# Feed-forward stage of a Mamba block: a written table of slots in place of the scheduler from the third group on, and an earlier place for W_down

## The chip, the core and the metric

The kernel runs on one core of one Trainium2 chip. The metric is the device time of one execution in microseconds (us), where lower is better; the time before is the median of three runs.

## The reference

The block takes 8192 rows of 512 values. The first part is a Mamba layer (a scan over a state of 16 per channel); the change does not touch it. The second part is a feed-forward network whose inputs and weights are rounded to a 4-bit grid (FP4) in blocks of 16, each block with its own scale:

```python
def fp4_quant_dequant(x):            # BLOCK = 16, along the last axis
    scale = jnp.maximum(jnp.max(jnp.abs(xb), axis=-1, keepdims=True) / 6.0, 1e-12)
    xn = xb / scale
    idx = jnp.searchsorted(_MID, jnp.abs(xn))
    return (_GRID[idx] * jnp.sign(xn) * scale).reshape(shape)
...
h = _layernorm(x, axis=-1) * (1 + cb) + sb      # x: 8192 x 512
gate = fp4_linear(h, w_gate)                    # 512 -> 1408
y    = fp4_linear(h, w_up)
x = x + gb * fp4_linear(silu(gate) * y, w_down) # 1408 -> 512
```

## The kernel before

The Mamba layer takes the first two thirds of the time. Its last rows are written to a DRAM buffer `mo`, one of 16 pieces of 512 rows, and the feed-forward stage reads them from there.

The feed-forward stage works in 16 **groups** of 512 rows (`n` from 0 to 15). The 1408 hidden channels are 11 blocks of 128 (`NF` = 11), and these are taken in four **parts** of 3, 3, 3 and 2 blocks (`PARTS`, `FPB` = 3). The tiles hold fp32. For each group:

- `load` and `head` (lines 910 to 927), four times, one for each 128 rows: two loads on the queue of SyncE (SP), the residual sum on GpSimd (POOL), the sums of a layer norm on VectorE (DVE), a power on POOL, the scaling on DVE, two multiply-adds with the modulation on POOL, and then the four steps of the rounding helper `_fp4_steps`: `scales` (DVE: maximum of a block, scale, reciprocal, multiply), `leads` (ScalarE, ACT: two passes), `rounds` (DVE: four passes) and `values` (POOL: multiply by the scale).
- `turn` (line 938), four times: four 128x128 transposes on TensorE (PE), and a copy by ACT into `xqT`, the group's input with channels on the partitions.
- `up` (line 966), eleven times: four matmuls for the gate and four for the other half, into the PSUM tiles `pg` and `pu` (two buffers each); ACT's Silu of `pg`, DVE's product with `pu`, and DVE's transpose within 32x32 blocks into `ht`.
- `quantize` (line 981), four times, one for each part: the same rounding steps on up to 1536 columns, and at the end, in `back`, DVE's transpose into `hT` (line 989). The last part has 1024 columns.
- `down` (line 993), four times: eleven matmuls of `hT` with `wd` into `po`, DVE's sum with the residual (line 1004) and the store.

`quantize_down` rounds a row block of W_down (128 x 1408; four of them, with a row scale `gc` that carries the output gate) and `turn_down` transposes it into `wd`, once, during groups 0 and 1.

One program text issues all this, and for this stage the order on each engine is chosen by the framework's scheduler, by its own estimates and the order of the text as priority. What the text says is that the steps of part `c` are spread over the `up` calls of part `c`+1, that the heads of group `n`+1 are issued with parts 0 and 1 of group `n`, and that the four `down` calls of group `n`-1 come after the **first part** (three `up` calls) of group `n`:

```python
if n > 0 and c == (1 if n == 1 else 0):
    for j in range(NJ):
        down(n - 1, j)
```

The Mamba layer, in contrast, has a written order (`tc.manual_schedule()`), in which each engine executes its instructions as the text issues them.

Of the kernel before, what the change touches and what calls it, by code (L numbers as in the profile page):

```python
# [8 lines left out]
F32 = mybir.dt.float32  # L9
# [12 lines left out]
def _layernorm(nc, small, src, dst, mhalf):  # L22

    st = small.tile([P, 6], F32, tag="st", name="st")
    nc.vector.bn_stats(st, src)
    mv = small.tile([P, 2], F32, tag="mv", name="mv")
    nc.vector.bn_aggr(mv, st)
    ve = small.tile([P, 1], F32, tag="ve", name="ve")
    nc.vector.tensor_scalar(ve, mv[:, 1:2], EPS, None, ALU.add)
    rstd = small.tile([P, 1], F32, tag="rstd", name="rstd")  # L30
    nc.gpsimd.tensor_tensor(rstd, ve, mhalf, ALU.pow)
    nc.vector.tensor_scalar(dst, src, mv[:, 0:1], rstd, ALU.subtract, ALU.mult)
# [69 lines left out]
def mamba_then_fp4_ffn(  # L102
# [768 lines left out]
    with ExitStack() as fa:  # L871
# [3 lines left out]
        FPB = 3  # L875
        PARTS = [(f, min(FPB, NF - f)) for f in range(0, NF, FPB)]
        wq2 = pool("wq2", 1)
        wd = wq2.tile([P, NF, DM], F32, tag="wd", name="wd")
        gc = wq2.tile([P, NK], F32, tag="gc", name="gc")
        hTp = pool("hTp", len(PARTS) + 1)  # L880
        wide = pool("wide", 1)
        work = pool("fwork", 1)
        io = pool("fio", 2 * NJ + 2)
        xqp = pool("xqp", 2)
        fsm = pool("fsm", 2)
        wq = pool("wq", 1, side="right")
# [4 lines left out]
        wu = wq.tile([P, NK, FF], F32, tag="wu", name="wu")  # L891
        sb = wq.tile([P, DM], F32, tag="sb", name="sb")
# [14 lines left out]
        head_work = Wide(work, DM, ("xn", "e"))  # L907
        xts2, xqT, hTs, todo, turned = {}, {}, {}, [], []

        def load(t):  # L910
            xt = io.tile([P, DM], F32, tag="x1", name=f"x1_{t}")
            nc.sync.dma_start(xt, mo[t // NJ][t % NJ * P : (t % NJ + 1) * P, :])
            h2 = work.tile([P, DM], F32, tag="h2", name=f"h2_{t}", bufs=2)
            nc.sync.dma_start(h2, x[t * P : (t + 1) * P, :])
            xts2[t] = xt, h2

        def head(t):

            xt, h2 = xts2[t]
            nc.gpsimd.tensor_tensor(xt, xt, h2, ALU.add)  # L920
            _layernorm(nc, small, xt, h2, mhalf)
            nc.gpsimd.tensor_tensor(h2, h2, cb1, ALU.mult)
            nc.gpsimd.tensor_tensor(h2, h2, sb, ALU.add)
            *steps, values = _fp4_steps(nc, head_work, fsm, h2, None, DM, slope0, nc.vector)
            for step in steps:
                step()
            xts2[t] = xt, values()
# [18 lines left out]

        def quantize_down(r):
            raw = wide.tile([P, FF], F32, tag="wraw", name=f"wraw_{r}")
            nc.sync.dma_start(raw, w_down[r * P : (r + 1) * P, :])

            *steps, values = _fp4_steps(
                nc, rows_work, fsm, raw, None, FF, slope0, nc.gpsimd, gc[:, r : r + 1]
            )

            def keep():
                turned.append((r, values()))

            return [*steps, keep]

        def turn_down():  # L960
            for r, q in turned:
                transposed(q, NF, lambda b0, nb, pt: nc.scalar.activation(
                    wd[:, b0 : b0 + nb, r * P : (r + 1) * P], pt[:, :nb, :], AF.Copy))
            turned.clear()

        def up(n, f, ht, i):
# [9 lines left out]
            g = wide.tile([P, T], F32, tag="g", name=f"g_{n}_{f}", bufs=3)  # L976
# [4 lines left out]
        def quantize(n, c, ht):  # L981
# [3 lines left out]

            def back():
                xn = values()
                hT = hTs[n, c] = hTp.tile([P, FPB * T], F32, tag="hT", name=f"hT_{n}_{c}")
                nc.vector.transpose(hT[:, :w], xn)  # L989

            return [*steps, back]

        def down(n, j):
            t = n * NJ + j
            po = pdn.tile([P, DM], F32, tag="po", name=f"po2_{t}")
            for c, (f0, nb) in enumerate(PARTS):
                for i in range(nb):
                    o = i * T + j * P
                    nc.tensor.matmul(  # L999
                        po, lhsT=hTs[n, c][:, o : o + P], rhs=wd[:, f0 + i, :],  # L1000
                        start=(f0 + i == 0), stop=(f0 + i == NF - 1),
                    )
            xt = xts2.pop(t)
            nc.vector.tensor_tensor(xt, xt, po, ALU.add)
            nc.sync.dma_start(out[t * P : (t + 1) * P, :], xt)

        nc.sync.dma_start(sb, rows[0:1, :].partition_broadcast(P))
        nc.sync.dma_start(cb1, rows[1:2, :].partition_broadcast(P))
        for t in range(NJ):
            load(t)  # L1010
            head(t)
            turn(t)
        for f0, nb in PARTS:
# [3 lines left out]
        nc.sync.dma_start(gc, rows[2:3, :].rearrange("o (r p) -> p (o r)", p=P))  # L1017
        NQ = L // T
        for n in range(NQ):
            for c, (f0, nb) in enumerate(PARTS):  # L1020
                ht = wide.tile([P, FPB * T], F32, tag="ht", name=f"ht_{n}_{c}", bufs=2)
# [5 lines left out]
                turn_down()  # L1027
                todo += quantize(n, c, ht)
                r = n * len(PARTS) + c - 1
                if 0 <= r < NK:  # L1030
                    todo += quantize_down(r)
                if n + 1 < NQ and 0 < c < 3:
                    for j in (2 * c - 2, 2 * c - 1):
                        turn((n + 1) * NJ + j)

                if n > 0 and c == (1 if n == 1 else 0):
                    for j in range(NJ):
                        down(n - 1, j)
                if n + 1 < NQ and c < 2:
                    for j in (2 * c, 2 * c + 1):  # L1040
                        load((n + 1) * NJ + j)
                        head((n + 1) * NJ + j)
        for step in todo:
            step()
        for j in range(NJ):
            down(NQ - 1, j)
# [40 lines left out]
```

## Time and profile before

| | us |
|---|---|
| median of 3 runs (lowest, highest) | 5899.88 (5898.19, 5905.25) |
| the profiled execution, its own time | 5902.15 |
| its span, first to last instruction | 5900.3 |
| first matmul of the feed-forward stage's group 0 | at 3920.88 |
| end of the `down` calls of group 1 | at 4230.12 |
| end of the `down` calls of group 13 | at 5685.27 |
| end of the `down` calls of group 14 | at 5800.32 |

Mean granted TensorE clock of the execution: 0.951. In the profile a matmul in fp32 shows as two instructions, each of a pitch of 0.429 us for a 128x512 tile, so that one `up` is 16 instructions and one `down` is 22. A line of the timeline gives the start, the duration, engine, source line, operation, output and inputs, the count, and in brackets the idle time before it with what ended it. The timeline merges neighbours, and the duration of a merged piece runs to the end of its last instruction, 0.17 us after the next one starts. Line numbers are those of the kernel before.

### The profile page before, as it was taken

Reading aid. Unit: us, or ns where it says so; the run is one execution under the profiler, and the core shown is the slowest. Engines: PE = TensorE matmul, PEld = TensorE weight load, DVE = VectorE, ACT = ScalarE, POOL = GpSimd, SP = SyncE. Lnnn points to the kernel's source line nnn. Section 1 sums busy time; section 2 is a strip of 40 time slices with the busy share of each in tenths; the row PEclk is TensorE's granted clock in tenths of the full one; section 3 lists DMA queues with packets and bytes.
Section 4 is the critical chain, followed back from the end, with each engine's and each line's share of the span. In section 5 each row is a group of like instructions: output and inputs, shape, how many; then the busy total and the mean of one; then the engine's idle time right before and its main releaser. Section 6 shows DMA issues by size and latency. Waiting matters only on the chain.

```text
span 5900.3 us, 58295 instructions
## 1 busy us (share of the span) xinstructions
PE 5272.3 (89%) x19812; PEld 3083.6 (52%) x19812; DVE 5079.0 (86%) x5219; ACT 2985.6 (51%) x5512; POOL 4205.3 (71%) x2419
## 2 busy tenths in 40 slices
PE   7788889889889888898898888788999999999999
PEld 4555556555555655565556555543444444444444
DVE  7999999999999999999999999977777667776674
ACT  6676666776676667667766665522212122211221
POOL 4999999999999999999999999953322323232320
PEclk9999999999999899999999999889999999999999
DMA  5444444444444444444444444430100000000000
GB/s 182 154 155 151 157 152 159 153 154 152 155 158 151 150 157 155 152 154 157 159 153 152 156 150 153 150 113 24 34 22 27 31 28 22 23 27 32 25 15 14
DMA packets 221985, 659.40 MB, mean 112 GB/s; under 512 B 24915, under 2 KB 40403, under 8 KB 221686
## 3 DMA queue, kind: packets, MB, share of 16 engines
q1 hardware_dynamic: 221110, 654.63, 34.1%
q8 instruction: 155, 2.54, 0.2%
q14 instruction: 144, 1.18, 0.1%
q10 hardware_dynamic: 576, 1.05, 0.0%
HBM read 615.22 MB, written 40.38 MB: 111 GB/s over the span
## 4 chain that ended last, share of the span: by engine, by line
DVE 35%; PE 26%; POOL 19%; ACT 10%; issue 9%; DMA 1%; DVEq 0%; POOLq 0%; SPq 0%; ACTq 0%
DVE da L502 13%; POOL db L466 9%; PE po L999 6%; ACT da L476 5%; POOL hp L518 4%; PE pg L972 4%; PE pu L972 4%; DVE hc L526 3%; DVE hp L502 3%; PE po L426 3%; PE y L395 2%; PE cv L271 2%; DVE e L82 2%; PE pz L369 2%; DVE xn L84 2%
## 5 line engine op out<-in xcount | busy, mean ns | idle before, releaser
L466 POOL TENSOR_TENSOR db<-bc,du 128x1024 f32<-128x1024 f32 x1024 | 2395.8, 2362 | 38.0 <-DVE da L502 31.7
L502 DVE TENSOR_TENSOR_SCAN da<-da,state,db 128x512 f32<-128x512 f32 x1280 | 1644.7, 1285 | 91.2 <-ACT da L476 38.1
L476 ACT ACTIVATE da<-delta,na 128x512 f32<-128x512 f32 x2048 | 1407.6, 689 | 427.1 <-DVE hc L526 294.2
L502 DVE TENSOR_TENSOR_SCAN hp<-da,state,db 128x512 f32<-128x512 f32 x768 | 940.8, 1266 | 47.1 <-ACT state L499 27.6
L395 PE MATMUL y<-ident,hc 128*128 128x128 f32 x5120 | 740.0, 294 | 225.9 <-DVE hc L526 184.2
L518 POOL TENSOR_TENSOR hp<-hp,bc 128x1024 f32<-128x1024 f32 x384 | 905.5, 2358 | 30.7
L90 POOL TENSOR_TENSOR xn<-xn,sc 128x512 f32<-128x512 f32 (+3 forms) x144 | 274.8, 1908 | 905.8 <-DVE xn L85 874.2
L395 PEld LDWEIGHTS y<-ident,hc 128*128 128x128 f32 x5120 | 635.1, 151 | 398.4 <-DVE hc L526 245.2
L526 DVE TENSOR_TENSOR hc<-da,bc 128x1024 f32<-128x1024 f32 x640 | 781.3, 1221 | 25.3 <-issue 0.5
L999 PE MATMUL po<-wd,hT 128*128 128x512 f32 x1408 | 636.2, 612 | 57.0 <-DVE hT L989 56.5
L972 PE MATMUL pg<-xqT,wg 128*128 128x512 f32 x1408 | 637.7, 595 | 1.7 <-ACT xqT L943 1.7
L972 PE MATMUL pu<-xqT,wu 128*128 128x512 f32 x1408 | 634.2, 593 | 0.0
L977 ACT ACTIVATE g<-pg 128x512 f32<-128x512 f32 x176 | 102.8, 592 | 833.6 <-PE pg L972 827.3
L369 PE MATMUL pz<-w_in,hT 128*128 128x256 f32 x2048 | 484.4, 391 | 32.7 <-DVE z L384 27.7
L271 PE MATMUL cv<-hT,w_in 128*128 128x512 f32 x1024 | 479.2, 612 | 31.2 <-ACT delta L350 15.8
L999 PEld LDWEIGHTS po<-wd,hT 128*128 128x128 f32 x1408 | 273.8, 196 | 415.5 <-issue 337.0
L426 PE MATMUL po<-w_o,xc 128*128 128x512 f32 x1024 | 463.0, 601 | 18.9 <-DVE z L384 12.2
L299 PE MATMUL cv<-raw,taps 128*128 128x512 f32 x1024 | 467.8, 599 | 12.8 <-ACT taps L285 12.8
L395 PE MATMUL y<-ident,hp 128*128 128x128 f32 x3072 | 447.6, 294 | 27.5 <-POOL hp L518 27.5
L76 ACT ACTIVATE a<-xn 128x512 f32<-128x512 f32 (+3 forms) x144 | 144.5, 1011 | 633.3 <-DVE xn L72 590.1
L395 PEld LDWEIGHTS y<-ident,hp 128*128 128x128 f32 x3072 | 391.9, 153 | 114.7 <-issue 47.7
L972 PEld LDWEIGHTS pu<-xqT,wu 128*128 128x128 f32 x1408 | 267.5, 190 | 335.4 <-issue 327.4
(112 smaller groups left out, 6195.9 us busy)
## 6 DMA issues: line engine op xcount, KB each, us to landing
bc<-bc SPq DMA_DIRECT2D x1024, 512.0 KB, 4.5
x<-in_x_dram SPq DMA_DIRECT2D x64, 256.0 KB, 4.8
h<-in_x_dram SPq DMA_DIRECT2D x64, 256.0 KB, 2.7
x<-mo SPq DMA_DIRECT2D x64, 256.0 KB, 2.7
out_dram<-x SPq DMA_DIRECT2D x64, 256.0 KB, 2.0
mo<-po SPq DMA_DIRECT2D x60, 256.0 KB, 2.2
w_in<-in_w_inT_dram SPq DMA_DIRECT2D x2, 2048.0 KB, 9.2
wm<-in_wmod_dram SPq DMA_DIRECT2D x8, 512.0 KB, 4.4
```

The source lines that it names most:

```text
L271: nc.tensor.matmul(ps, lhsT=w_in[:, f, o : o + P], rhs=hT[k][:, f, :], start=(f == 0), stop=(f == NK - 1),)
L299: nc.tensor.matmul(v, lhsT=taps[:, i, :], rhs=raw[:, i : i + T], start=(i == 0), stop=(i == 3))
L369: nc.tensor.matmul(pz[:, b, :], lhsT=hT[k][:, f, t0 : t0 + P], rhs=w_in[:, f, o : o + DH * P], start=(b == 0 and f == 0), stop=(f == NK - ...
L395: nc.tensor.matmul(y[:, j, i * P : (i + 1) * P], lhsT=src[:, j * P : (j + 1) * P], rhs=ident, start=start and j % 2 == 0, stop=stop, is_tr ...
L426: nc.tensor.matmul(pend["po", k, j], lhsT=xcs[k, d][:, j * P : (j + 1) * P], rhs=w_o[:, d, :], start=(d == 0), stop=(d == ND - 1),)
L466: nc.gpsimd.tensor_tensor(db, bct[slot // DH, 0], dus[k, h, i].unsqueeze(1).to_broadcast([P, GN, T]), ALU.mult)
L476: nc.scalar.activation(pend["da", slot][:, q, :], deltas[k, h][:, i, :], AF.Exp, scale=na[:, d, n : n + 1])
L502: nc.vector.tensor_tensor_scan(to[:, q, :], da[:, q, :], db[:, q, :], state[:, d, n : n + 1], ALU.mult, ALU.add,)
L518: nc.gpsimd.tensor_tensor(to, to, c_rows, ALU.mult)
L526: nc.vector.tensor_tensor(hc, hs, c_rows, ALU.mult)
L972: nc.tensor.matmul(ps, lhsT=wt[:, k, f * P : (f + 1) * P], rhs=xqT[n][:, k, :], start=(k == 0), stop=(k == NK - 1),)
L999: nc.tensor.matmul(po, lhsT=hTs[n, c][:, o : o + P], rhs=wd[:, f0 + i, :], start=(f0 + i == 0), stop=(f0 + i == NF - 1),)
```

## The change

From the third group on (`n` >= 2) the stage has a written order. A group has 15 **slots**: eleven `up` calls, and the four `down` calls of the group before in slots 5 to 8 (`SPLIT` = 5; in the last group they come last). A table says in which slot each other step is issued, after the slot's `up` or `down`; a step's slot may lie in the next group's first five slots. `S`, `L`, `R` and `B` are the steps of a part (scales, leads, rounds with values, and the transpose into `hT`), `n`, `m`, `s`, `l`, `r`, `t` those of a head (residual and norm sums, scaling and modulation, scales, leads, rounds with values, `turn`).

Further: a head's steps for two row blocks alternate (`beside`); its rounded values are written over `h2`, which has four buffers; layer norm is cut in two steps; the residual tile has 11 buffers where it had 10, the Silu's output `g` two where it had three; `hT` has four buffers for the first three parts and one for the last. W_down's row blocks 0 and 1 are loaded behind the first weights and rounded beside group 0's first part (it was blocks 0 to 2 beside parts 1 to 3 of group 0, and block 3 beside part 0 of group 1), and `turn_down` follows a part later. At the end the last group's `down` calls for row blocks 0 and 1 take the parts in turn.

```diff
+        SPLIT, LOADS = 5, (1, 1, 1, 6)
+        PART_STEPS = {"S": (0,), "L": (1,), "R": (2, 3), "B": (4,)}
+        HEAD_STEPS = {"n": (0,), "m": (1,), "s": (2,), "l": (3,), "r": (4, 5)}
+        BESIDE = (4, 5, 6, 7), (10, 11, 12, 14), (13, 14, 15, 17), (16, 17, 18, 19)
+        ENDING = (4, 5, 6, 7), (7, 8, 9, 15), (10, 11, 12, 15), (15, 16, 17, 18)
+        HEADS = 2 * ((5, 6, 7, 7, 8, 11),) + 2 * ((7, 8, 9, 10, 11, 14),)
...
-        hTp = pool("hTp", len(PARTS) + 1)
+        gp = pool("gp", 2)
+        rowsp = pool("rowsp", 3)
+        hTp = pool("hTp", 1)
-        io = pool("fio", 2 * NJ + 2)
+        io = pool("fio", 3 * NJ - 1)
+        hsm = pool("hsm", NJ)
...
         for t in range(NJ):
             load(t)
-            head(t)
-            turn(t)
+        load_down(0)
+        load_weights(0)
+        load_down(1)
+        for c in every[1:]:
+            load_weights(c)
+        beside(head(0), head(1))
+        turn(0)
+        turn(1)
+        beside(head(2), head(3))
+        turn(2)
+        turn(3)
+        todo += quantize_down(0)
+        todo += quantize_down(1)
...
-                turn_down()
-                todo += quantize(n, c, ht)
-                r = n * len(PARTS) + c - 1
-                if 0 <= r < NK:
-                    todo += quantize_down(r)
+                turn_down(ahead)
+                ahead = len(turned)
+                if (n, c) != (1, LAST):
+                    todo += quantize(n, c, ht)
+                if n == 0 and c < 2:
+                    load_down(c + 2)
+                    todo += quantize_down(c + 2)
...
-        for step in todo:
-            step()
-        for j in range(NJ):
-            down(NQ - 1, j)
+        fa.enter_context(tc.manual_schedule())
+        NS = NF + NJ
...
+        for n in range(2, NQ):
+            split = SPLIT if n + 1 < NQ else NF
+            hts = {}
+            for q in range(NS):
+                steps = steps_at.pop(n * NS + q, ())
+                for step in steps:
+                    if step[0] == "t":
+                        do(*step)
+                if split <= q < split + NJ:
+                    down(n - 1, q - split, every)
+                else:
+                    f = q if q < split else q - NJ
+                    c, i = divmod(f, FPB)
...
+                    up(n, f, hts[c], i)
...
+                for step in steps:
+                    if step[0] != "t":
+                        do(*step)
...
+        for some in (every[:1], every[1:2], every[2:3], every[3:]):
+            for j in range(2):
+                down(n, j, some)
+        for j in range(2, NJ):
+            down(n, j, every)
```

## The prediction

> **What bounds the kernel now.** I read the slices of the page first, then the groups, then the timeline of PE between two groups, and last the busy times by stage.
>
> ```profile
> PE   7788889889889888898898888788999999999999
> PEclk9999999999999899999999999889999999999999
> ...
> L999 PE MATMUL po<-wd,hT 128*128 128x512 f32 x1408 | 636.2, 612 | 57.0 <-DVE hT L989 56.5
> ```
>
> The feed-forward stage fills the last 14 slices. In 12 of them PE is over 90% busy, and the only matmuls of the stage with much idle time before them are those of `down`: 57.0 us, waiting for L989, the transpose into `hT`. PE is the bound; what can be won is its pauses. The timeline of PE at one boundary, and then the line of DVE that ends the pause:
>
> ```profile
> 4425.02 3.60 PE L972 MATMUL pu<-xqT,wu 128*128 128x512 f32 x8
> 4428.45 7.89 PE L999 MATMUL po<-wd,hT 128*128 128x512 f32 x18
> 4440.32 33.18 PE L999 MATMUL po<-wd,hT 128*128 128x512 f32 x70 [3.98 <-DVE hT L989]
> 4473.34 3.60 PE L972 MATMUL pg<-xqT,wg 128*128 128x512 f32 x8
> ```
> ```profile
> 4439.04 1.23 DVE L989 STREAM_TRANSPOSE hT<-xn 128x1024 f32<-128x1024 f32 x1
> ```
>
> PE does 18 instructions of `down` (nine matmuls: parts 0 to 2), then stands 3.98 us until the last part's `hT` is there at 4440.27. Afterwards 70 instructions take 33.0 us instead of 70 x 0.429 = 30.0: the granted clock is lower behind the pause. Stage by stage (columns: length, busy PE, PEld, DVE, ACT, POOL, granted clock):
>
> ```profile
> 3920.88:4230.12 309.24, 268.54 (x652) 122.98 (x653) 240.07 (x286) 75.14 (x90) 115.97 (x67) 0.93 0.09 27
> 4230.12:5685.27 1455.15, 1407.11 (x3362) 627.84 (x3361) 1046.18 (x1318) 295.09 (x372) 439.01 (x288) 0.98 0.08 26
> 5685.27:5800.32 115.05, 115.05 (x281) 51.81 (x281) 70.26 (x77) 22.42 (x27) 15.56 (x9) 1.00 0.03 12
> 5800.32:5900.30 99.98, 93.23 (x216) 40.52 (x215) 48.09 (x48) 13.11 (x14) 7.55 (x3) 1.00 0.03 13
> ```
>
> The second row is 12 groups of 121.26 us each. The third is one group in which PE never waited: 115.05, at clock 1.00. It checks by count: 11 `up` x 6.87 + 4 `down` x 9.44 + 4 `turn` x 0.435 = 115.1.
>
> **Part 1: the steady groups.** `down` moves from behind three `up` calls to behind five. The last part's rounding then has two more `up` slots, 13.7 us, against a pause of 4. By the table, counted from the group's start: `R` of the last part is issued in slot 3; DVE reaches it after that slot's product and transpose (0.68 + 0.70), at 27.5 + 0.2 + 1.4 = 29.1, needs 1.23 + 0.65 + 1.22 + 1.22 = 4.3 and ends at 33.4; POOL's multiply (2.25) ends at 35.7; `B` (1.23) comes behind slot 4's `up` and ends at 37.2. The first `down` starts at 34.3 and needs it after nine matmuls, 7.7 us later: 42.0. Margin 4.8 us. So the excess of 121.26 over 115.05, 6.21 us (4 of pause, 2 of clock), goes in all 12 groups: **74.6 us**.
>
> What may be late next is DVE, now in a fixed order. Its work by slot, from the rows of one group: an `up` 1.38, a `down` 0.66, `S` 4.42, `R` 7.15, `B` 1.78 (3.13, 4.32, 1.23 for the last part), a head's `n` 1.0, `m` 0.54, `s` 1.86, `r` 3.04. Slots 0 and 12 come to 8.5 us against a slot of 6.87, slot 11 to 7.5, slot 4 to 7.0; their neighbours have 3 to 6, so DVE falls at most 2.3 us behind (after slot 12) and has caught up by slot 14. PE feels a lag only when an `up`'s product is not done before the matmuls of the second `up` after it fill the same `pu` buffer, 6.87 + 3.43 = 10.3 us later. The `turn` of rows 2 and 3, slot 14 (at 107.3): `r` is DVE work of slot 11, done at 93.6 + 0.2 + 7.5 = 101.3, POOL 1.07, so 102.4; margin 5. The fourth head's load stands on SP behind the store of the second `down` (53.9), lands 2.7 later, and `n` runs after slot 7's `down` (62.7): margin 6. Queued behind that store on SP are only this head's two loads and the next two stores, which nobody waits for before the next group. The extra `hT` and residual buffers cost nothing; two `g` buffers in place of three neither, since a Silu comes 10.3 us after the `up` whose buffer it takes.
>
> DVE and POOL slow each other, though. POOL's multiply L922 has a least time of 1.26 us, a median of 1.27 and a longest of 2.73, which fell beside DVE passes of 1536 columns. One group's 87.2 us of DVE and 37.3 of POOL have the present share of that in them. Taken from both sides: none of POOL's time is added to DVE (87.2 of 115.05), or all of it is (124.5, more than the period). I take the first, as the same work in 121.2 us leaves DVE 28% idle; the second is the rival below.
>
> The Trainium skill (SBUF — State Buffer, "Who interferes with whom") says that DVE instructions with two SBUF inputs and GpSimd instructions that read SBUF exclude one another for a whole instruction. It speaks against a table that puts heads beside parts; by it the period would lie nearer to the second value than I take it.
>
> **Part 2: groups 0 and 1.** The first window holds, for PE, 25 `up` (171.7), 8 `down` (75.5), 8 `turn` (3.5) and W_down's 44 transposes (4.8): 255.5. It took 309.2, so 53.7 are lost: 40.7 of pauses in the timeline (12.5 and 8.3 the longest, mostly for POOL's L90, W_down's and the heads' values) and 13 of clock. After the change the order of each queue can be listed. Three of W_down's four rows are now turned within group 0 and the fourth in the second `up` of group 1 (before: from the end of group 0 to the tenth `up` of group 1). Up to the last pass of the fourth row DVE has, from the first `up` on: 4 rows x 8.4 = 33.5, two parts 26.7, a third part's scales 4.4, three and a half heads 22.5, ten products with transposes 13.8: 101 us. DVE was busy 91% of the time in 3950 to 4100, so 111, and POOL's multiply 2.9: 114. PE has 12.6 `up`, 33 transposes and four `turn` there: 92. So 22 idle. From there to heads 8 and 9: DVE 36 / 0.91 + 1.1 = 40.7 against PE's 31.5: 9 more. Then DVE has slack. With 3 for ACT's copies of W_down through two `pt` buffers it is 34 of pauses, and clock in the old proportion (13 / 40.7), 10: 44. Gain **10 us**; bounds 53.7 (no pause) and -10 (one more wait such as the 12.5).
>
> **Part 3: the two ends.** Before group 0 the loads of `x` for rows 2 and 3 no longer wait for a buffer (they were issued at 3880.86), so the pauses of 5.87 and 3.59 before the third and fourth `turn` shrink; but the four residual sums now stand on POOL ahead of the first head's modulation (two more, 1.27 each). Between -3 and +9.5; I take **2**, near the lower end, since the same PE matmuls of the Mamba layer still follow the first `turn`. At the end, after group 14's last `down`, DVE has the sum 0.66, `B` of parts 1 and 2 3.6, `S` 3.1, `R` 4.3, `B` 1.2, ACT 2.2 and POOL 1.9: 17.1, some 17.7 with hand-overs; PE has 18 matmuls of parts 0 to 2 in that time, 15.4. A pause of 2.3, for 0.79 + 2.40 before: gain **1**.
>
> **Sum.** 74.6 + 10 + 2 + 1 = 87.6. The profiled execution took 5902.15 by its own time (span 5900.3 and 1.85 around it), 2.3 over the median of the runs. 5902.15 - 87.6 = 5814.6, forecast **5815**.
>
> **The rivals.**
> *A wait in the place of the old one.* The heads' values come late and the `turn` of slot 14 (or 11) waits in every group, by DVE's and POOL's fixed order. With the smallest pause of the end stage, 2.4, and 2 of clock, 13 groups give 57: 5872. For it: POOL's two modulations of each head sit between DVE steps. Against: margin 5. Chance 0.12.
> *Slower.* DVE becomes the bound because POOL's instructions hold it up for their full length: 124.5 a group, 13 x (124.5 - 115.05) = 123, so 5938. It is slower than before from the point where more than 121.26 - 87.2 = 34 of POOL's 37.3 us are added. Against: L922's median is its undisturbed time. Chance 0.06.
> *The clock falls when PE no longer pauses.* At 0.98 over 1600 us that is 32: 5847. Against: the third window, 115 us without a pause at 1.00. Chance 0.05.
> *The early stage loses its pauses altogether*: 41 more, 5774. Against: DVE's sum. Chance 0.04.
>
> **How the numbers follow.** 0.73 is left for the forecast, whose own range is 5800 to 5835 (start -3 to +9.5, groups 0 and 1 some 12 either way). To leave out no more than 2 in 10 the range goes up to the first rival: 5795 to 5876. A measurement of this kernel can tell about 0.2%, 12 us. Slower by more 0.06, within 0.01 (a case between the first two rivals), faster 0.93.
>
> **What would show it.** In the changed kernel's profile: periods of 115.1 between the `down` calls of neighbouring groups, no idle time before L1043 (the matmuls of `down`) for `hT`, granted clock 1.00 from group 2 on; 40 to 50 lost before group 2; a pause of 2 to 3 before the last part's matmuls at the end. Wrong would be: pauses before L968 (`turn`) in every group, DVE over 95% busy there, or a period above 117.

## The result, and the profile after

The changed kernel takes 5800.18 us (median of four runs, 5799.56 to 5805.17) against 5899.03 beside it on the same chip: ratio 0.9834, 95% interval 0.9817 to 0.9851. The forecast was 5815 within 5795 to 5876. The profiled execution took 5800.66, span 5798.8, mean granted clock 0.955 (before 0.951).

The page of the changed kernel: the slices of PE and of its clock, and the group of `down`'s matmuls (L999 is now L1043; `turn`'s L935 is L968, `up`'s L972 is L1009).

```profile
PE   7789889888898898888988988768999999999999
PEclk9989999999999999999998999889999999999999
...
L1043 PE MATMUL po<-wd,hT 128*128 128x512 f32 x1408 | 608.5, 593 | 2.0 <-DVE hT L1029 2.0
```

The 57.0 us of idle time before `down` are 2.0, and one of its instructions takes 593 ns in the mean in place of 612: both the pause and the slower clock behind it are gone. The timeline of PE at one boundary shows how:

```profile
4407.08 3.60 PE L1009 MATMUL pu<-xqT,wu 128*128 128x512 f32 x8
4410.51 37.93 PE L1043 MATMUL po<-wd,hT 128*128 128x512 f32 x88
```

All 88 instructions of the four `down` calls come in one piece, where before there were 18, a pause of 3.98 and 70 slower ones. The busy times by stage (columns: length, busy PE, PEld, DVE, ACT, POOL, granted clock, DMA share, GB/s): from the first `up` to the end of group 1's `down`, then twelve groups and a piece, then the end, and last one period by itself:

```profile
3912.18:4218.18 306.00, 281.07 (x685) 127.79 (x686) 243.56 (x273) 75.13 (x91) 106.65 (x59) 0.96 0.07 24
4218.18:5600.46 1382.28, 1382.28 (x3365) 622.52 (x3364) 1111.04 (x1323) 301.89 (x374) 404.43 (x290) 1.00 0.08 28
5600.46:5798.80 198.34, 192.78 (x461) 85.74 (x459) 125.69 (x135) 34.16 (x39) 29.52 (x17) 1.00 0.03 12
4295.46:4410.51 115.05, 115.05 (x281) 51.81 (x280) 92.57 (x110) 25.08 (x31) 33.62 (x25) 1.00 0.08 28
```

In the second row PE is busy for the whole length, at clock 1.00; the period is 115.05. VectorE, which the prediction feared next, is at 92.6 of 115. The end (the 52 instructions from the last part's on) waits 2.04 us:

```profile
5772.70 22.58 PE L1043 MATMUL po<-wd,hT 128*128 128x512 f32 x52 [2.04 <-DVE hT L1029]
```

Where the 101.5 us between the two spans (5900.3 and 5798.8) came from:

| | before | after | gain | predicted |
|---|---|---|---|---|
| last matmul of the Mamba scan (`y`, L395, now L402) | 3869.56 | 3866.71 | 2.9 | not named |
| from there to the first `up` | 51.3 | 45.5 | 5.8 | 2 |
| first `up` to the end of group 1's `down`: lost beyond PE's need (309.24 - 255.5; 306.0 - 269.2, as there are 27 `up` in it, not 25) | 53.7 | 36.8 | 16.9 | 10 |
| from there to PE's last matmul: lost beyond its need | 78.4 | 2.4 | 76.0 | 74.6 + 1 |

The remaining -0.1 is the store at the end. Against the forecast of 5814.6 the profiled execution is 13.9 shorter, which is 2.9 of the first row, 3.8 of the second, 6.9 of the third and 0.3 of the last two. The 2.9 can't be put down to the change: in the 14 executions profiled here that matmul begins anywhere between 3861.4 and 3872.2, with the same text ahead of it, and at 3866.71 and 3864.93 in two executions of the changed kernel. So two kernels are compared below by their ratio and, where less than 0.3% matters, by the time from that matmul to the end of the span: 2030.7 before, 1932.1 and 1932.4 after.

### The profile page after: what moved, and what is told of

It is laid out like the page before. It is cut to its first block, busy times and chain, and to the rows that moved or that the text cites. A ratio compares the mean times of both kernels' runs of the same rounds, so it can differ in the third digit from the quotient of the medians.

```text
span 5798.8 us, 58407 instructions
## 1 busy us (share of the span) xinstructions
PE 5244.5 (90%) x19812; PEld 3077.0 (53%) x19812; DVE 5153.1 (89%) x5219; ACT 2991.1 (52%) x5512; POOL 4168.0 (72%) x2419
## 4 chain that ended last, share of the span: by engine, by line
PE 42%; DVE 24%; POOL 18%; ACT 9%; issue 8%; DMA 0%; DVEq 0%; POOLq 0%; SPq 0%; ACTq 0%
DVE da L509 12%; PE po L1043 10%; POOL db L473 10%; PE pu L1009 9%; PE pg L1009 9%; POOL hp L525 5%; ACT da L483 4%; DVE hc L533 3%; DVE hp L509 3%; PE po L433 3%; PE y L402 2%; PE cv L278 2%; PE pz L376 2%; PE cv L306 1%; POOL du L365 1%
## 5 line engine op out<-in xcount | busy, mean ns | idle before, releaser
L402 PE MATMUL y<-ident,hc 128*128 128x128 f32 x5120 | 737.7, 293 | 223.8 <-DVE hc L533 183.1
L402 PEld LDWEIGHTS y<-ident,hc 128*128 128x128 f32 x5120 | 633.1, 151 | 396.7 <-DVE hc L533 245.2
L97 POOL TENSOR_TENSOR xn<-xn,sc 128x1536 f32<-128x1536 f32 (+2 forms) x80 | 200.6, 2507 | 852.1 <-DVE xn L92 844.7
L1009 PE MATMUL pu<-xqT,wu 128*128 128x512 f32 x1408 | 637.0, 595 | 5.9 <-DVE g L1015 5.9
L1009 PE MATMUL pg<-xqT,wg 128*128 128x512 f32 x1408 | 634.9, 593 | 1.5 <-ACT g L1014 0.8
L1043 PE MATMUL po<-wd,hT 128*128 128x512 f32 x1408 | 608.5, 593 | 2.0 <-DVE hT L1029 2.0
L83 ACT ACTIVATE a<-xn 128x512 f32<-128x512 f32 (+2 forms) x144 | 145.7, 1012 | 869.5 <-DVE xn L79 834.8
L402 PE MATMUL y<-ident,hp 128*128 128x128 f32 x3072 | 449.2, 295 | 27.6 <-POOL hp L525 27.6
L402 PEld LDWEIGHTS y<-ident,hp 128*128 128x128 f32 x3072 | 393.5, 154 | 114.1 <-issue 50.0
L1009 PEld LDWEIGHTS pu<-xqT,wu 128*128 128x128 f32 x1408 | 267.8, 191 | 343.7 <-issue 323.5
L1043 PEld LDWEIGHTS po<-wd,hT 128*128 128x128 f32 x1408 | 268.0, 190 | 339.6 <-issue 330.4
L376 PEld LDWEIGHTS pz<-w_in,hT 128*128 128x128 f32 x2048 | 393.2, 197 | 93.1 <-DVE z L391 32.2
```

What stands on the lines that cost most here:

```text
L376: nc.tensor.matmul(pz[:, b, :], lhsT=hT[k][:, f, t0 : t0 + P], rhs=w_in[:, f, o : o + DH * P], start=(b == 0 and f == 0), stop=(f == NK - ...
L402: nc.tensor.matmul(y[:, j, i * P : (i + 1) * P], lhsT=src[:, j * P : (j + 1) * P], rhs=ident, start=start and j % 2 == 0, stop=stop, is_tr ...
L1009: nc.tensor.matmul(ps, lhsT=wt[:, k, f * P : (f + 1) * P], rhs=xqT[n][:, k, :], start=(k == 0), stop=(k == NK - 1),)
L1043: nc.tensor.matmul(pos[j], lhsT=hTs[n, c][:, o : o + P], rhs=wd[:, f0 + i, :], start=(f0 + i == 0), stop=(f0 + i == NF - 1),)
```

## The experiments

The theory: the pause of PE at every group's `down` goes since `down` is issued two `up` calls later **and** the table keeps VectorE's and POOL's other work from making something else late; VectorE has room; the early stage gains since W_down is ready earlier. The rivals: the place of `down` alone, the order alone, or a VectorE or POOL that is close to being the bound.

| kernel | median, us | ratio to before (95%) | from the last `y` to the end |
|---|---|---|---|
| `down` one part later, nothing else | 5881.89 | 0.9965 (0.9952 to 0.9978) | 2013.7 |
| table, `down` at its old place | 5926.56 | 1.0043 (1.0028 to 1.0058) | 2057.5 |
| after, products turned twice | 5804.44 | 0.9836 (0.9822 to 0.9851) | 1934.4 |
| after, products turned four times | 5946.66 | 1.0077 (1.0060 to 1.0094) | 2081.3 |
| after, heads' values six times | 6134.30 | 1.0393 (1.0375 to 1.0410) | 2259.1 |
| after, 75 short POOL instructions a period | 5803.09 | 0.9830 (0.9813 to 0.9846) | 1938.9 |
| after, W_down at its old places | 5803.72 | 0.9836 (0.9822 to 0.9849) | 1939.2 |
| after, first four heads one by one | 5796.78 | 0.9825 (0.9812 to 0.9839) | 1932.3 |
| after, heads of groups 1 and 2 one by one | 5804.86 | 0.9830 (0.9816 to 0.9845) | 1935.2 |
| after, W_down's rows 2 and 3 a part later | 5799.29 | 0.9829 (0.9816 to 0.9842) | 1928.5 |
| after, once more | 5799.44 | 0.9829 (0.9816 to 0.9843) | 1932.4 |
| after, table from group 1 on | 5792.65 | 0.9813 (0.9798 to 0.9827) | 1924.0 |

### The place of `down` alone

```diff
-                if n > 0 and c == (1 if n == 1 else 0):
+                if n > 0 and c == 1:
```

> The kernel before with one edit: in every group down comes one part later (after the second part, as group 1 has it already); the scheduler still orders all engines and W_down, heads and buffers are as they were. Theory 1 (the record's): a steady period lost 4 us to the wait for hT and 2 us of clock behind it; with down later that wait goes, but the scheduler's order of VectorE's queue lets another wait come up, for the product of the gate that frees pu, so that the period is 116 to 119 us and the whole 5826 to 5874 (middle 118: 5899 - 12 x 3.2 = 5861). Rival: the place of down is everything in the steady groups and the table adds nothing; period 115.0 to 115.6, whole 5826 to 5832. Second rival: the scheduler had down early for a reason, and the wait only changes its name (turn behind POOL's values); period 120 to 122, whole 5885 to 5905.

Measured: 5881.89, a gain of 18 us of the 99. The period is 119.7 (two `down` calls in a row at 4449.74 and 4569.45). The page and the timeline of PE:

```profile
L972 PE MATMUL pu<-xqT,wu 128*128 128x512 f32 x1408 | 656.6, 610 | 35.1 <-DVE g L978 35.0
...
L999 PE MATMUL po<-wd,hT 128*128 128x512 f32 x1408 | 609.3, 594 | 3.2 <-DVE hT L989 3.2
```
```profile
4387.82 5.40 PE L972 MATMUL pu<-xqT,wu 128*128 128x512 f32 x8 [2.68 <-DVE g L978]
```

The wait for `hT` is gone as completely as in the changed kernel (3.2 us in the whole run), and another one stands in its place: PE waits 2.7 us a period for the gate's product, which must read `pu` before it is written again, and then runs eight instructions in 5.40 us that take 3.60 at full clock. VectorE's timeline shows what the product stands behind:

```profile
4378.25 2.45 DVE L82 SCALAR_TENSOR_TENSOR e<-a,e 128x1536 f32<-128x1536 f32 x1
...
4384.47 2.70 DVE L85 SCALAR_TENSOR_TENSOR xn<-e,xn 128x1536 f32<-128x1536 f32 x1
4387.10 0.67 DVE L978 TENSOR_TENSOR g<-g,pu 128x512 f32<-128x512 f32 x1
```

The scheduler put a whole part's rounding, 8.8 us, ahead of it. So the first theory had the right wait, but its size was too small: 2.7 of pause and 1.8 of clock, 4.6 over 115.05, for a range that ended at 4 (and at 5874 for the whole). The rival that the place is everything falls; the second rival's ranges begin at 120 and 5885, just above.

### The table with `down` at its old place

```diff
-        SPLIT, LOADS = 5, (1, 1, 1, 6)
...
-        BESIDE = (4, 5, 6, 7), (10, 11, 12, 14), (13, 14, 15, 17), (16, 17, 18, 19)
+        SPLIT, LOADS = 3, (1, 1, 1, 6)
...
+        BESIDE = (4, 5, 6, 7), (10, 11, 12, 14), (13, 14, 15, 17), (15, 16, 16, 17)
```

> The changed kernel with the table kept but down at its old place, after the first part (slots 3 to 6 of each group; the last part's four steps one slot earlier so that hT can be there at all). Theory: the wait for hT comes back at 4 us or more a period, with up to 2 us of clock behind it, and with the turns of the next group one or two waits besides; period 120 to 125, whole 5860 to 5920. Rival: the order of the queues is what gained, and the table hides the wait even with down early: period 115 to 117, whole 5800 to 5824.

Measured: 5926.56, slower than the kernel before, and 7 above the theory's range; the period is 125.1 (mean of eleven), just above its upper end of 125. One period of PE, its pauses only:

```profile
4363.34 0.66 PE L968 MATMUL pt<-ident,h 128*128 128x128 f32 x4 [0.22 <-POOL h L97]
4366.45 0.75 PE L968 MATMUL pt<-ident,h 128*128 128x128 f32 x4 [2.45 <-POOL h L97]
4426.48 32.88 PE L1043 MATMUL po<-wd,hT 128*128 128x512 f32 x76 [3.58 <-DVE hT L1029]
```

The wait for `hT` is back at 3.57 to 3.95, and two turns wait for POOL besides. It is not quite the old wait: PE does 12 instructions of `down` ahead of it, not 18, so it's the third part's `hT` that is late. VectorE makes it at 4424.69, behind the last part's rounding, which the edit moved two slots earlier while the third part's `B` kept its slot. The turns' wait I put down to the heads' steps of slots 7 and 8, which now stand behind an `up` with its product on VectorE, where they stood beside a `down`; no run takes it apart. A fixed order is only as good as its slots; this one is worse than the scheduler's, and what a table laid out for the old place would give, no run shows. So neither half, as tried here, gains much alone: 18 us and -26 us against 99 together.

### Room on VectorE

```diff
-            nc.vector.transpose(ht[:, i * T : (i + 1) * T], g)
+            for _ in range(2 if n > 1 else 1):       # and 4 in the second kernel
+                nc.vector.transpose(ht[:, i * T : (i + 1) * T], g)
```

> The changed kernel with every transpose of a gate's product done twice from the third group on: 11 more VectorE instructions of 0.711 us a period, spread evenly, so 7.8 us on top of VectorE's 92.6 of 115.0. Theory: VectorE has 22.5 us of room a period and it is spread over the slots; period 115.0 to 115.6, whole 5800 to 5808. Rival: the margins lie within single slots (PE waited 2.9 us in 132 slots for the product already), and a longer slot on VectorE shows at once; period 117 to 119, whole 5825 to 5850.

> The changed kernel with every transpose of a gate's product done four times from the third group on: 33 more VectorE instructions of 0.711 us a period, 23.5 us, so VectorE would need 116.0 us of a period of 115.0. Theory that only the sum over a period counts: period 116 to 118, whole 5812 to 5836. Theory that slots with a part's rounding, a head's and a product fill up first, while others still have room, and that the TensorE clock falls behind the pauses: period 121 to 129, whole 5870 to 5970.

Busy times in one period of each (columns as above; once more, then three times more):

```profile
4299.05:4414.10 115.05, 115.05 (x281) 51.81 (x280) 99.99 (x121) 24.96 (x31) 33.60 (x24) 1.00 0.09 28
```
```profile
4433.98:4560.23 126.25, 118.95 (x281) 52.84 (x280) 114.83 (x144) 25.07 (x31) 33.58 (x24) 0.97 0.07 25
```

With 7.4 us more on VectorE the period doesn't change in the second decimal: at 100.0 of 115.05 nothing of it is on PE's path. With 22.3 more the period is 126.25, although VectorE would fit into 115.05 by its sum (114.83): the theory of the whole period's sum falls, that of the slots holds. The pauses of one period, from the timeline of PE (`down` is L1044 in this kernel):

```profile
4390.58 0.66 PE L968 MATMUL pt<-ident,h 128*128 128x128 f32 x4 [2.28 <-POOL h L97]
4446.88 31.81 PE L1044 MATMUL po<-wd,hT 128*128 128x512 f32 x70 [5.01 <-DVE hT L1030]
```

The two margins that the prediction named are what gives way, `hT` and the turn of slot 14.

### Room on POOL, and what VectorE pays for it

First the last step of each head, six times:

```diff
-            xts2[t] = xt, values()
+            xts2[t] = xt, values(6 if t >= 3 * NJ else 1)
```

> The changed kernel with POOL's last step of every head (values, 512 columns, 1.334 us at the median) done six times from the third group's rows on: 20 more POOL instructions a period, 26.7 us, POOL 60 of 115 us. It tests the rival on record that VectorE stands still while POOL works. Theory: POOL holds VectorE up for a part of its time only, as the two traces suggest (VectorE 87.2 to 92.6 us a period when the table laid heads beside parts, POOL 33.6): VectorE's busy time rises by 3 to 10 us, stays below 103, and the period stays 115.0 to 115.6; whole 5800 to 5808. Rival: VectorE pays for the full length, 26.7 us more, 119.2 us a period; the period is then 119.5 or more and the whole 5850 or more. A third possibility that is no matter of VectorE: the turns, three slots behind, wait for POOL; then PE pauses before L968 (here one line further down, L969) while VectorE is below 103.

Measured: 6134.30, far above the theory's range and inside the rival's, which is open upwards. One period, and two of PE's four pauses in it (lines stand one further down in this kernel, `turn` at L969):

```profile
4744.36:4884.35 139.99, 120.22 (x281) 53.79 (x280) 99.38 (x110) 25.18 (x31) 62.19 (x45) 0.93 0.07 23
```
```profile
4803.58 1.12 PE L969 MATMUL pt<-ident,h 128*128 128x128 f32 x4 [6.03 <-POOL h L98]
4804.49 5.12 PE L1010 MATMUL pg<-xqT,wg 128*128 128x512 f32 x8
...
4840.32 1.12 PE L969 MATMUL pt<-ident,h 128*128 128x128 f32 x4 [9.53 <-POOL h L98]
4841.23 5.52 PE L1010 MATMUL pg<-xqT,wg 128*128 128x512 f32 x8
```

VectorE rose by 6.8 us for 28.6 on POOL, to 99.4: within the theory's range, and no bound. What decided was the third possibility, the turns' wait for POOL: 0.87 + 6.03 + 3.35 + 9.53 = 19.8 of pauses, and 5.2 of clock, make the 25 us that the period grew (in the 5.2 are also the last 0.17 us of the matmuls ahead of each pause). The edit put its work on a chain with a small margin. How small, the changed kernel's own trace says (POOL, then PE):

```profile
4365.36 1.06 POOL L97 TENSOR_TENSOR h<-xn,sc 128x512 f32<-128x512 f32 x1 [1.88 <-DVE xn L92]
```
```profile
4368.44 1.04 PE L968 MATMUL pt<-ident,h 128*128 128x128 f32 x8
```

The second head's values end at 4366.42 and the two turns of slot 14 begin at 4368.44: 2.0 us of margin, where the prediction had 5. So POOL's room was asked for again, with instructions that nobody waits for:

```diff
+        spare = wq.tile([P, 96], F32, tag="spare", name="spare")
...
+                for _ in range(5 if n + 1 < NQ else 0):      # at the end of each slot
+                    nc.gpsimd.tensor_tensor(spare, cb1[:, :96], sb[:, :96], ALU.mult)
```

> The changed kernel with five POOL instructions of 96 columns more in every slot from the third group on but for the last, on a tile that nobody reads, so that no turn waits for them: 75 a period. From the rows of 2 columns (0.19 us) and 512 columns (1.05 us unhindered) one should last about 0.35 us, 26 us a period, POOL 60 of 115. It asks again what VectorE pays when POOL works more, without the wait for POOL that decided the run with the heads' values done six times (VectorE 92.6 to 99.4 us a period for 28.6 us more on POOL, 24 in the hundred). Theory: VectorE rises by 4 to 10 us, stays below 103, the period stays 115.0 to 115.6; whole 5799 to 5808. Rival on record: full length; VectorE at 118 us or more of 115, period 118.6 or more, whole 5843 or more.

The added instructions in one period, as a group and by their durations (least, median and longest, in ns), and the busy times:

```profile
L1168 POOL TENSOR_TENSOR spare<-cb,sb 128x96 f32<-128x96 f32 x75 | 41.3, 551 | 5.2
```
```profile
L1168 POOL TENSOR_TENSOR spare<-cb,sb x75: 384/389/1988, 4298.1 to 4404.6; 128x96 f32<-128x96 f32 x75
```
```profile
4296.92:4411.98 115.06, 115.06 (x282) 51.90 (x281) 93.61 (x110) 25.09 (x31) 75.65 (x100) 1.00 0.08 28
```

POOL is at 75.7 of 115 instead of 60, VectorE pays 1.0 us, and the period stands. (The 6.8 us that its last column in the table is over the changed kernel's lie ahead of the end of group 1's `down`: the scheduler put 15 of the added instructions at 3874.0 to 3886.9, beside the first heads.) The rival on record, that POOL holds VectorE up for its full length, is refuted twice: 1.0 for 42 us, 6.8 for 28.6.

The mean of 0.55 hides two kinds. 59 of the 75 took 0.39 us, near the 0.35 expected; the other 16 took 0.45 to 1.99. Each of these 16 ran beside a pass of the rounding steps on VectorE (L79, L89, L91 or L92, which read two tiles, and twice L90, which reads one) and ended 0.24 to 0.25 us behind that pass. Five in a row on POOL, and what VectorE did meanwhile:

```profile
4369.96 7.04 POOL L1168 TENSOR_TENSOR spare<-cb,sb 128x96 f32<-128x96 f32 x5
```
```profile
4370.14 1.83 DVE L89 SCALAR_TENSOR_TENSOR e<-a,e 128x1536 f32<-128x1536 f32 x1
...
4373.06 1.83 DVE L91 SCALAR_TENSOR_TENSOR xn<-e,xn 128x1536 f32<-128x1536 f32 x1
4374.92 1.83 DVE L92 SCALAR_TENSOR_TENSOR xn<-e,xn 128x1536 f32<-128x1536 f32 x1
```

So the two engines do shut each other out, one whole instruction at a time, and here POOL does most of the waiting: 12 of its 41.3 us. VectorE waits for at most one short instruction, and where its passes are longer beside the added instructions, it is by 0.07 to 0.23 us. Beside POOL's 512 columns, in the run with the heads' values six times, single passes went from 0.69 to 1.43 us and from 1.76 to 2.50.

The Trainium skill (SBUF — State Buffer, "Who interferes with whom") has DVE instructions with two SBUF inputs and GpSimd instructions that read SBUF exclude each other for a whole instruction. The trace agrees, by the ends of the 16. What the exclusion costs VectorE depends in these runs on how long the single POOL instruction is, and it is far from POOL's whole busy time.

### Groups 0 and 1, and the start

```diff
@@ W_down at its old places
-        load_down(0)
...
-        load_down(1)
...
-        todo += quantize_down(0)
-        todo += quantize_down(1)
...
-                turn_down(ahead)
-                ahead = len(turned)
...
-                if n == 0 and c < 2:
-                    load_down(c + 2)
-                    todo += quantize_down(c + 2)
+                turn_down(len(turned))
...
+                r = n * len(PARTS) + c - 1
+                if 0 <= r < NK:
+                    load_down(r)
+                    todo += quantize_down(r)
```

> The changed kernel with W_down's rows loaded, quantized and turned at their old places (beside parts 1 to 3 of group 0 and the first of group 1); the table and everything else stay. Theory 1: most of the 16.9 us that the stretch from the first up matmul to the end of down(1) gained (306.0 against 309.24 us with two ups more) comes from the earlier rows. Then that stretch lasts 316 to 323 us here, and the whole 5810 to 5817. Theory 2: it comes from down moving out of group 2's second slot and from the table, and the rows only change places with other waits. Then the stretch stays at 304 to 309 us and the whole at 5797 to 5804. In both the first up matmul comes at 3912 give or take 2 if its 8.7 us have nothing to do with W_down, and at 3918 to 3921 if the two rows worked on in the start are what brought it forward. The steady period stays 115.0.

Measured: from the last `y` to the end 1939.2, 7.0 more than the changed kernel. The second theory holds for the stretch: from the first `up` to the end of group 1's `down` it lasts 306.8 against 306.0 and 305.8, 1 us more and not 10. The first `up` came at 3913.90, where both theories had it if W_down plays no part, but only because this execution's Mamba stage ended early (3862.05). The way from `y` to the first `up` is 51.85 (45.5 and 45.9 after, 51.3 before). The timeline of PE ahead of the first `up` in this kernel:

```profile
3906.63 0.60 PE L968 MATMUL pt<-ident,h 128*128 128x128 f32 x4
3912.99 1.11 PE L968 MATMUL pt<-ident,h 128*128 128x128 f32 x4 [5.76 <-POOL h L97]
3913.90 4.84 PE L1009 MATMUL pg<-xqT,wg 128*128 128x512 f32 x8
```

The second line is the `turn` of row block 4, which belongs to group 1: without W_down's rows beside it the scheduler had its head so early that it put this turn ahead of the first `up`, and PE waited 5.76 us for it. In the changed kernel it stands behind. So the start's gain isn't W_down's earlier work as such, but what its steps displaced. For the same reason the 1 us of the stretch is too little: one of its heads had been done ahead of it. Counted from `y`, start and stretch together, W_down's place is worth 7 of the 22.7 us (5.8 and 16.9) that the changed kernel gained there.

```diff
@@ the first four heads one by one
-        beside(head(0), head(1))
-        turn(0)
-        turn(1)
-        beside(head(2), head(3))
-        turn(2)
-        turn(3)
+        for t in range(NJ):
+            beside(head(t))
+            turn(t)
@@ the heads of groups 1 and 2 one by one
                         load((n + 1) * NJ + j)
-                    beside(*(head((n + 1) * NJ + j) for j in (2 * c, 2 * c + 1)))
+                        beside(head((n + 1) * NJ + j))
```

> The changed kernel with the first four heads one by one again (head, turn, head, turn) in place of two heads side by side. Theory 1: the pairs are what brought the first up matmul from 3920.88 to 3912.18; then it returns to 3918 to 3921 and the whole is 5806 to 5809. Theory 2: the scheduler interleaves heads by itself, and the 8.7 us come from loads that no longer wait for a buffer and from the end of the stage ahead, which stands 2.9 to 4.4 us earlier; then the first up matmul comes at 3911 to 3914 and the whole within 3 us of 5800. The steady period stays 115.0.

> The changed kernel with the heads of groups 1 and 2 built one by one in the loop (load, head, load, head) in place of two side by side. Theory: the pause of 8.32 us that the kernel before had at 4155.03 before a turn that waits for POOL, and that the changed kernel no longer has, went because two heads are worked on side by side; one by one it returns, and the stretch from the first up matmul to the end of down(1) goes from 306.0 to 311 to 316 us, the whole to 5805 to 5810. Rival: what took it away is the table, which orders the turns' predecessors from group 2 on, and the larger buffers; stretch 304 to 308 and whole 5798 to 5803.

The first leaves everything as it was (1932.3; the first `up` 45.9 after `y`): the pairs are nothing to the scheduler at the start. In absolute times its first `up` came at 3907.58, earlier than either theory had it, because its Mamba stage ended earlier. The second is 3.0 longer, 1.1 of it in the stretch (307.0) and 1.7 in the last matmuls, which ran slower behind their pause of 2.04 (24.28 us for 22.58). The pause of 8.32 at 4155 that I expected back did not come back: the rival holds, though the median of 5804.86 lies between the two ranges.

```diff
@@ W_down's rows 2 and 3 a part later
-                if n == 0 and c < 2:
-                    load_down(c + 2)
-                    todo += quantize_down(c + 2)
+                if n == 0 and 1 <= c < 3:
+                    load_down(c + 1)
+                    todo += quantize_down(c + 1)
@@ the table from group 1 on
-        for n in range(2):
+        for n in range(1):
...
-        for n in range(2, NQ):       # twice; the last part of group 0, not 1, goes with them
+        for n in range(1, NQ):
```

> The changed kernel with W_down's rows 2 and 3 loaded and quantized one part later each (beside the second and third part of group 0 rather than the first and second). A candidate for a better version. Theory 1: the 8.10 us pause before the turn of W_down in group 0, where ScalarE's copies stand behind a head's leads that wait for VectorE, is caused by too many quantizations at once; spread out, the stretch from the first up matmul to the end of down(1) falls from 306.0 to 297 to 301 us and the whole to 5791 to 5796. Theory 2: the pauses only move, stretch and whole within 3 us of before the edit (303 to 309; 5797 to 5803).

> The changed kernel again, unchanged, beside the other kernels of this set, for comparison on one chip: 5800 give or take 2 us, first up matmul at 3912, stretch to the end of down(1) 306 us, period 115.0.

> The changed kernel with the table from the second group on rather than the third: group 0 alone is left to the scheduler, the second group's down of group 0, its heads and its parts come at the same slots as in every later group. Theory: the pauses of the second group (5.49 us before a turn that waits for POOL, 1.9 before a product) and half of what the stretch still loses come from the scheduler's order there, and the table takes them away as it does later; the pauses of group 0 stay. The whole is 5788 to 5794 (8 us less than the changed kernel's 5800). Rival: in the second group the end of W_down's work is still queued, and the table's fixed order runs into it; whole 5800 to 5815.

Rows 2 and 3 later: the stretch is 301.9, 3.9 less than the changed kernel beside it (the first theory had 5 to 9), with 5.57 in place of 8.10 for the pause before W_down's turn and 10.60 in place of 4.3 for a later one, but without the 5.48 before the turn of heads 8 and 9. The time itself, 5799.29 against 5799.44, doesn't show it. The changed kernel once more came as expected.

The table from group 1 on: 1924.0 from `y` to the end, 8.2 less than the changed kernel (mean of two); between the first `up` and the end of group 2's `down` it takes 412.5 against 421.0. PE after W_down's last turn:

```profile
4026.92 1.91 PE L968 MATMUL pt<-ident,xn 128*128 128x128 f32 x8 [0.47 <-POOL xn L97]
4052.17 37.93 PE L1043 MATMUL po<-wd,hT 128*128 128x512 f32 x88
4167.22 37.93 PE L1043 MATMUL po<-wd,hT 128*128 128x512 f32 x88
```

Group 1 already runs at 115.05 from its `down` on, and the pause of 5.49 and the clock behind it are gone, as the theory had it. The pause of 1.9 before a product, which it named as well, stayed: 2.49 at 4024.78, in the second group. The kernel's median of 5792.65 is below that of before and of the changed kernel; the interval of its ratio (0.9798 to 0.9827) overlaps that of the changed kernel, so the timed runs alone don't show the 8 us; the trace does.

## Why the prediction was right, and which steps were not

**The steady groups: right in mechanism and size.** Period 115.05 for 115.05, clock 1.00, 76.0 us for 74.6 + 1. The margin of the last part's `hT`, 4.8 by the sum, is 4.9 in the trace: its transpose ends at 4413.34, and the 18 instructions that can run without it end 7.7 after 4410.51. The experiments add that this took both halves of the change, which the sum over slots had implied: `down` later without the order gave 18 us, the order without `down` later, in the one table tried, lost 26.

**The turn's margin: mis-sized.** 5 was predicted for slot 14, 2.0 was there. The sum for slot 11 did hold the rounding of both heads (7.5 us). What it had too small is how late VectorE comes to that slot: it took 2.3 us at most, after slot 12, but the products of slots 9 to 12 begin 4.5, 5.1, 3.2 and 3.4 us behind the end of their matmuls. The lateness comes from the `down` slots ahead of them, where each engine waits for the other. VectorE's timeline, with the product of slot 10, whose matmuls had ended at 4347.13, as the last line:

```profile
4321.40 3.49 DVE L37 TENSOR_SCALAR h<-x,mv,rstd 128x512 f32<-128x512 f32 x2
...
4335.67 0.69 DVE L28 BATCH_NORM_STATS2 st<-x 128x6 f32<-128x512 f32 x1 [1.90 <-POOL x L942]
...
4352.24 0.68 DVE L1015 TENSOR_TENSOR g<-g,pu 128x512 f32<-128x512 f32 x1
```

Two scalings of heads took 3.49 us, where the sum has 1.1, and the fourth head's norm waited for POOL's residual sum: it began 74.5 us into the group, where the step has 62.7 with a margin of 6. So the second head's rounding and multiply in slot 11 come 3.3 us behind the first's (on POOL 4362.04 and 4365.36), and only the first's end where the step had both. The first rival (a wait at this turn) was therefore nearer than its chance of 0.12 was argued from; a POOL or VectorE 2 us slower would have brought it in, and turning every product four times did.

**VectorE.** I took 87.2 us a period and none of POOL's time; it is 92.6. The difference lies in a few rows: the scaling of a head, its blocks' scale multiply and its blocks' small pass. One of them, before and then after:

```profile
L32 DVE TENSOR_SCALAR h<-x,mv,rstd 128x512 f32<-128x512 f32 x4 | 2.2, 541 | 4.5 <-POOL rstd L31 4.5
```
```profile
L37 DVE TENSOR_SCALAR h<-x,mv,rstd 128x512 f32<-128x512 f32 x4 | 5.2, 1348 | 0.0
```

The passes of 1536 columns fell in return (L82's 2.04 to L89's 1.73), and POOL went from 36.6 (mean of twelve groups; 37.3 in the one above) to 33.6. So the table moved where the two engines meet; VectorE paid 5.4 us for it, out of 28 that it had. The longest of these scalings, 3.03 us for the 0.54 it takes by itself, ended 0.28 behind a multiply on POOL that lasted from 4321.62 to 4324.60. Taking none of POOL's time was too low, then, and all of it (37.3) far too high.

**Groups 0 and 1: the sum right in size, not in its terms.** 36.8 are lost, 44 were predicted: 24.9 of pauses for 34, 11.9 of clock for 10. Up to W_down's last turn the pauses are 19.4 for 25, before heads 8 and 9 5.5 for 9; and ACT's copies of W_down, a side term of 3, ended the longest pause of all, 8.10. The step that failed is the attribution: it credited W_down's earlier place with the gain. Put back, it costs 1 us there, and 7 of 22.7 with the start; the heads one by one cost 1.1; `down` later alone leaves 52.8 of the 53.7 lost by the same count (328.93 with 28 `up`). What went are the two pauses that the kernel before has after 4150, 8.32 before a turn and 5.77 before `down`, with the clock behind them; in the kernels with the table in which only W_down's rows or the heads are edited PE doesn't pause between 4100 and the end of group 1's `down`. Whether it is the order of the first slots of group 2, the last part of group 1 that is issued in them, or the additional buffers of `h2` and of the rounding that took the 8.32 away, no run separates.

**The start: mis-sized.** 5.8 where 2 was taken (and 9.5 was the bound). The two pauses of 5.87 and 3.59 didn't shrink but vanished, since the loads of all four row blocks are early; the price is not the residual sums on POOL that the step charged, but a new pause of 4.97 to 7.30 where PE's output projection of the Mamba layer waits for ACT's copy of `po`, queued behind the heads' leads. And the step didn't ask which turn stands ahead of the first `up`, which is what W_down's place decides.

**The end: right**, 2.04 for 2.3.

## What to carry to other kernels

When a wait at one place costs every iteration, moving the consumer later is half of the work: look which instruction on the producer's engine will be the last one in time next, and write the order down so that it isn't a long step ahead of a short one that others wait for. A bound by sums over a period is not enough where the order is fixed: VectorE at 115 of 115 by its sum already cost 11 us a period, so margins have to be worked out chain by chain, for the second of two interleaved chains too, and with the lateness that each engine brings from the slots before. And when the stage ahead ends several microseconds earlier or later from one execution to the next, measure small changes from the last instruction ahead of them, not from the start.

## What the runs showed of the hardware

- Looked at in short stretches, the granted clock of these traces is 1.00 or 0.50, and it is 0.50 in stretches of 3.41 us or a multiple of it; the price of a pause is half of the time that PE works in such a stretch. Behind the pause of 2.68 (`down` later) it is 0.50 from 4388.40 to 4391.81, and eight instructions took 5.40 us for 3.60. Behind 9.53 (heads' values six times) it is 0.50 from 4831.44 to 4845.09, but most of that is the pause itself; PE worked in 4.77 of it and lost 2.4. In the run with `down` later 2.67 to 2.82 us cost 1.6 to 1.8 in ten groups, 4.39 cost 1.8, and 3.34, with a stretch of 6.83, cost 3.0.
  Single pauses of 0.74 to 1.08 cost 0.1 (3.70 for eight instructions). Around 2 us it goes either way: behind the same last pause of 2.04, 52 instructions took 22.58 in the changed kernel and 24.28 with the heads of groups 1 and 2 one by one, where the clock is 0.50 from 5769.44 to 5772.85.
  The Trainium skill (TensorE: Matmul & The Clock Gate, "What's actually happening") has TensorE's clock at half after an idle window of about 3.4 us, until a window of that length has been busy, and the windows run freely, whenever the kernel starts. An estimate from that page: one window at half rate costs 1.7 us, however long the pause. The length, the half rate and the price that comes or fails with the same pause agree; the 3.0 behind 3.34 and the 2.4 behind 9.53 took more than one such window. But the window ahead need not be idle throughout: in the 3.41 us before 4388.40 (`down` later) PE was busy for 0.73, and in those before 5769.44 (heads one by one) for 1.37.
- A POOL multiply of 96 columns took 0.39 us, and up to 1.99 where it began beside one of VectorE's passes with two tile inputs (75 instructions added a period). 41.3 us of them cost VectorE 1.0; 28.6 us more on POOL, nearly all of 512 columns, cost it 6.8.
- The end of the Mamba stage moves by up to 10.8 us between executions (3861.4 to 3872.2 for its last `y` matmul) although that stage's text is the same in all of them.
